# Turning normalised rows on TensorE instead of by DMA transpose, with a new opening, in a transformer block of two FFNs around attention

## The chip, the cores and the metric

The kernel runs on one core of one Trainium2 chip. The metric is device time in microseconds (us), measured over whole executions; the median of three runs of the kernel before is 693.76 us. One execution was also taken with the hardware profiler. Its span, from the first to the last instruction, is a little shorter than its time.

The engines are named as in the profile: PE is TensorE (matmuls; PEld is its weight loads), DVE is VectorE, ACT is ScalarE, POOL is GpSimd, and SP is SyncE, which here only issues DMAs.

## What is computed

The input x has 32 batches of 256 rows with 128 features. The reference, cut to its steps:

```
x = x + 0.5 * ffn(layernorm(x))
x = x + attn(layernorm(x))
x = x + 0.5 * ffn(layernorm(x))

ffn(h):   h = concat([h, -h]);  h = s0 * (h @ sign(k0));  h = 2 * relu(h)
          h = s1 * (h @ sign(k1));  h = 2 * relu(h);  return s2 * (h @ sign(k2))
attn(h):  Q, K, V = h @ W.T + b  in 16 heads of 8 features
          ctx = softmax(Q K^T / sqrt(8)) V
          return layernorm(ctx + h) * gamma + beta
```

Here sign(k) is +1 where the boolean k is true and -1 elsewhere, and the hidden widths are 512 and 512. The result is float32. Products keep its precision by splitting each operand in a float16 high part and a float16 low part, and adding two or three products.

## The kernel before

**Units and stages.** The rows are cut into 16 units of two batches: 512 rows, held as a tile of 128 partitions by 4 row groups by 128 features. Each unit passes through ffn0 (`first`), the attention norm (`norm_attn`), the projections (`project`), and per batch the score maxima (`maxima`), their transport (`shift`), the weighted sum (`weigh`) and the end of attention (`context`), and then ffn1 (`second`; the last unit does it in two halves).

**Normalising and turning.** `normalize` (L544) computes row statistics on VectorE (L557, L558), the inverse root on POOL (L559, L561), and then subtracts and multiplies, on VectorE if `quick` (L566) and else on POOL (L571, L572). `turned` (L574) makes the turned tile xT, with features on partitions, in two float16 parts. If `quick`, TensorE transposes float32 row groups into PSUM (L585), ACT casts the high part (L588) and VectorE subtracts for the low part (L589). Else ACT casts (L593) and POOL subtracts (L594) first, and SP issues one DMA transpose of both parts (L595). The quick path is used for ffn0 of units 0 and 1 (QF = 2), the attention norm of unit 0 (QK = 1), and ffn1 of units 14 and 15 (QL = 2).

**Feed-forward.** `ffn` makes two hidden layers of four blocks and an output. Each block's product lands in one of three PSUM buffers named "m", which the projections, the transposes and the context share. `relu_split` (L618) evicts it: ACT writes the high part (L625), VectorE the low part (L626); or ACT writes a float32 copy (L628) and POOL subtracts (L623). The last residual addition is on VectorE (L678) or on ACT and POOL (L679, L680).

**Attention.** `project` (L709) makes Q and K (L384 to L386, evictions L728 and L730) and places them by DMA through DRAM (L733, L738) in a tile where a head has 8 of 32 partitions, three rows of parts and a fourth row for the shift. Q is a fresh tile for each unit, and its fourth row of 32 partitions is first filled with zeros by DMA from a DRAM tile (L717). `maxima` runs score matmuls (L781) and takes the row maxima on VectorE (L792). `shift` (L796) splits the maxima in a float16 high part (L802) and low part (L803) on VectorE, TensorE turns them (L809), ACT copies them (L814), and two DMAs put them in Q's fourth row (L815, L816), so that the second score product (L849) has the shift in it. ACT takes the exponential (L861), TensorE multiplies by V and a column of ones (L831), and `context` turns the result (L875), divides (L887, L888), adds, normalises and adds to x (L890 to L895, on VectorE if `quick`, else on POOL).

**The order of the work.** `_Plan` sets it. Every operation is recorded with an engine, an estimated cost and a rank, and `simulate` (L154) plays the engines against each other and writes the order of each engine's queue. TensorE takes its groups by rank and may skip ahead by SKIP or SKIP0. Score products of a batch and weighted ones of an earlier batch with the same rank run together. The array is used in three tilings: "D" (128x128), "C" (four blocks of 32 columns) and "R" (four blocks of 32 rows, for scores). Dense products (`dense`, L380) can run in "D" or "C" and take the tiling that is in use. `relief` (L259) moves a low part from VectorE to ACT and POOL where the simulation says that it ends sooner. A unit's stages have ranks at a distance of UNIT = 16 between units, with offsets: B0 for ffn0, BA for the attention norm, BP for the projections, BW for the weighted sums, B1 for ffn1, and AHEAD for how far a norm precedes its products. The loads of x are on SP at ranks two units ahead (L608).

**The opening.** x of unit 0 is loaded in halves, then the scalars, k0, k1, unit 1's x and k2. POOL sets the blank tiles of V and K to their constants (`blanks`, L530). The weights are unpacked on VectorE and ACT (`weights`, L406). `projections` (L454) scales, turns and splits the attention weights; the biases of Q and K are loaded a second time as rows (L476) and permuted on POOL (L490).

Of the kernel before, what the change touches and what calls it, by code (L numbers as in the profile page):

```python
# [55 lines left out]
PT, NHL, NXN = 5, 3, 5  # L56
# [3 lines left out]
QL = 2  # L60
# [5 lines left out]
B0, BA, BP, BW, BV, B1 = -34, -12.449, -7.379, 13, 4, 42.542  # L66

S0, S1 = 0.0, -1.082

BB = 2.143  # L70

RUSH, AHEAD = 0.378, 4.629

SKIP0, SKIP, UNTIL = 30.226, 3.003, 20.423

FAR = 37.851
# [3 lines left out]
WAIT = 0.12  # L80
# [8 lines left out]
BIAS = 0.6  # L89
# [18 lines left out]
class _Node:  # L108
    __slots__ = ("n", "eng", "cost", "emit", "rank", "kind", "rows", "lag", "needs", "then", "bufs", "count", "avail", "start", "tiling", "alt", "rush")


class _Plan:
# [11 lines left out]
    def op(self, eng, cost, emit, r=(), w=(), rank=0.0, kind="D", rows=0, lag=None, alt=None, rush=False):  # L124
# [3 lines left out]
        x.then, x.avail, x.start, x.rush = [], 0.0, None, rush  # L128
        needs = set()
# [24 lines left out]
    def simulate(self):  # L154
# [104 lines left out]
        def relief(now, best):  # L259

            nonlocal left
            for x in sorted((x for x in ready[DVE] if x.alt and x.avail <= now + 1e-9), key=lambda x: (x.rank, x.n)):
# [10 lines left out]
                y.rush, y.needs, y.then, y.bufs, y.count, y.avail, y.start = False, [], [x], [source, temp], 0, 0.0, None  # L273
# [18 lines left out]
            return None  # L292

        mode = "D"
        while left:
# [8 lines left out]
            while again:  # L304
                again = False
                for eng in range(5):
# [15 lines left out]
                    if group:  # L322
                        begin(group, now)
                        again = True
# [28 lines left out]
def tile_macaron(ctx: ExitStack, tc: tile.TileContext, x, Wq, bq, Wk, bk, Wv, bv, gamma, beta, k0, k1, k2, s0, s1, s2, out):  # L353
# [49 lines left out]
    op(POOL, 0.6, lambda: make_identity(nc, ident), w=["ident"], rank=-900)  # L403
    op(ACT, 1.58, lambda: nc.scalar.copy(ident16, ident), r=["ident"], w=["ident16"], rank=-850)

    def weights():  # L406
# [10 lines left out]
        sc1 = const.tile([P, 2], F32, name="sc1")  # L417
        for i, (src, e, eng) in enumerate(((s0, ACT, nc.scalar), (s1, SP, nc.sync), (s2, SP, nc.sync))):
            op(e, 0.5, lambda i=i, src=src, eng=eng: eng.dma_start(out=raw[:, i : i + 1], in_=src.partition_broadcast(P)),
               w=[("raw", i)], rank=-901, lag=3.2)  # L420
        op(ACT, 0.5, lambda: nc.scalar.dma_start(out=k0s.t, in_=k0.rearrange("(c p) f -> p c f", p=P)), w=[k0s], rank=-900, lag=2.6)
        op(ACT, 0.53, lambda: nc.scalar.dma_start(out=k1s.t, in_=k1.rearrange("(c p) f -> p c f", p=P)), w=[k1s], rank=-899, lag=3.2)
# [10 lines left out]
        for c in range(NF):  # L433
            if c < NF - 1:
                op(ACT, 0.7, lambda c=c: nc.scalar.activation(w1[:, c, :], k1s.t[:, c, :], AF.Identity, scale=sc1[:, 0:1], bias=sc1[:, 1:2]),
                   r=[k1s, "sc1a", "sc1b"], w=[("w1", c)], rank=-800)
            else:
                v(0.4, lambda c=c: nc.vector.tensor_scalar(w1[:, c, :], k1s.t[:, c, :], -0.5, sc1[:, 0:1], ALU.add, ALU.mult),
                  [k1s, "sc1a"], [("w1", c)])
        v(0.4, lambda: nc.vector.tensor_scalar(w2, k2s.t, 2.0, -1.0, ALU.mult, ALU.add), [k2s], ["w2"], B0 + 2)  # L440
        v(0.1, lambda: nc.vector.tensor_tensor(sab, raw, sgn, ALU.mult), [*raws, "sgn"], ["sab"], B0 + 2)
# [12 lines left out]
    def projections():  # L454
# [4 lines left out]
        br = const.tile([1, 2, 2, P], F32, name="br")  # L459
# [12 lines left out]
        for i, (W, b) in enumerate(((Wq, bq), (Wk, bk), (Wv, bv))):  # L472
            s(lambda i=i, W=W: nc.sync.dma_start(out=ws[:, i, :], in_=W), [("ws", i)])
            s(lambda i=i, b=b: nc.sync.dma_start(out=bn[:, i : i + 1], in_=b.rearrange("(f o) -> f o", o=1)), [("bn", i)])
            if i < 2:
                s(lambda i=i, b=b: nc.sync.dma_start(out=br[:, i, 0, :], in_=b.rearrange("(o f) -> o f", o=1)), [("br", i)])  # L476
# [5 lines left out]
        v(0.45, lambda: nc.vector.tensor_tensor(sq[:, :, 0:D], ws, ws, ALU.mult), wss, ["sq"])  # L482
        v(0.1, lambda: nc.vector.scalar_tensor_tensor(sq[:, :, D], bn, 1.0 / 128, bn, ALU.mult, ALU.mult), bns, ["sqb"])
# [8 lines left out]
        for i in range(2):  # L492
            op(POOL, 0.5, lambda i=i: permute(br[:, i, 1, :], br[:, i, 0, :], nc.gpsimd.tensor_copy), r=[("br", i)], w=[("brp", i)], rank=B0 + BB)
# [14 lines left out]
        def turn():  # L508
            for i in range(3):
                nc.tensor.transpose(pw.t[:, i, :], ws[:, i, :], ident)  # L510
            for i in range(2):
                nc.tensor.matmul(pw.t[:, 3, i : i + 1], br[:, i, 1, :], ones[0:1, 0:1], start=True, stop=True)

        op(PE, 0.7, turn, r=[*wss, "ident", ("brp", 0), ("brp", 1), "ones"], w=[pw], rank=B0 + BB + 0.3)
# [13 lines left out]
    nought = dram.tile([32, G, TU], F16, name="nought", bufs=1)  # L528

    def blanks():  # L530
        for j in range(NV):
            rank = j * UNIT + BP - 12
            op(POOL, 1.35, lambda j=j: nc.gpsimd.memset(vaug[j], 0.0), w=[("V", j)], rank=rank)
            op(POOL, 0.95, lambda j=j: nc.gpsimd.memset(ks[j].bitcast(I32), ONES), w=[("K", j, row) for row in range(4)], rank=rank)
# [5 lines left out]
        zero = buf(work, [32, G, TU], F16, "pt", PT, "zero")  # L540
# [3 lines left out]
    def normalize(dst, src, tag, n, rank, scale=1.0, quick=False):  # L544
# [7 lines left out]
        for a in range(0, n, step):  # L552
# [8 lines left out]
            op(POOL, 0.25 + 0.2 * step, lambda part=part: nc.gpsimd.tensor_tensor(rs.t[:, part, 0], ve.t[:, part], nhalf[:, part], ALU.pow),  # L561
# [12 lines left out]
    def turned(xn, tag, name, n, rank, quick):  # L574

        xT = buf(work, [P, 2, n * P], F16, f"xT{tag}", 2, f"xT{name}")
# [14 lines left out]
        else:  # L591
            hl = buf(work, [P, 2, n, D], F16, "hl", NHL, f"hl{name}")
            op(ACT, 0.52, lambda: nc.scalar.copy(hl.t[:, 0], xn.t), r=xns, w=[(hl, 0)], rank=rank)  # L593
            op(POOL, 1.12, lambda: nc.gpsimd.tensor_tensor(hl.t[:, 1], xn.t, hl.t[:, 0], ALU.subtract), r=[*xns, (hl, 0)], w=[(hl, 1)], rank=rank)  # L594
            op(SP, 1.35, lambda: nc.sync.dma_start_transpose(  # L595
                out=xT.t.rearrange("p a (t q) -> p (a t) q", q=P), in_=hl.t.rearrange("p a t d -> p (a t d)")),
               r=[(hl, 0), (hl, 1)], w=[(xT, i, a) for i in range(2) for a in range(0, n, 2)], rank=rank, lag=3.5)
        return xT

    xs, xns, qs, xTs, nms, cxs = {}, {}, {}, {}, {}, {}  # L600

    def load(u):
# [5 lines left out]
        e, eng, rank = (ACT, nc.scalar, -898) if u == 1 else (SP, nc.sync, (u - 2) * UNIT + B0)  # L608
        op(e, 0.5, lambda: eng.dma_start(out=b.t.rearrange("p (b c) d -> p b c d", b=2), in_=xu[u]), w=[(b, 0), (b, 2)], rank=rank, lag=2.7)


    def norm_ffn(key, src, n, rank, quick):
# [3 lines left out]
        xTs[key] = turned(xn, key[0][-1], name, n, rank, quick)  # L616

    def relu_split(hi, lo, m, ps, w, rank):  # L618
# [3 lines left out]
        def low(of):  # L622
            return lambda: nc.gpsimd.tensor_tensor(lo.t[:, m, :], of.t, hi.t[:, m, :], ALU.subtract)  # L623

        op(ACT, 0.09 + w / 1280, lambda: nc.scalar.activation(hi.t[:, m, :], ps.t, AF.Relu), r=[ps], w=[(hi, m)], rank=rank)  # L625
        op(DVE, 0.08 + w / 985, lambda: nc.vector.scalar_tensor_tensor(lo.t[:, m, :], ps.t, 0.0, hi.t[:, m, :], ALU.max, ALU.subtract),  # L626
           r=[ps, (hi, m)], w=[(lo, m)], rank=rank,
           alt=(0.09 + w / 1280, lambda: nc.scalar.activation(full.t, ps.t, AF.Relu), ps, full, 0.1 + w / 500, low(full)))  # L628

# [52 lines left out]

    def first(u):
        rank = u * UNIT + B0 + S0 * u / (NU - 1)
        norm_ffn(("ffn0", u), (xs[u], 0), NT, rank - AHEAD if u else -950, u < QF)
        ffn(("ffn0", u), (xs[u], 0), NT, rank, UNIT)

    def second(u, b):
        n, part = (NT, 0) if b is None else (2, 2 * b)
        rank = u * UNIT + B1 + S1 * u / (NU - 1) + (b or 0) * UNIT / 2  # L690
        norm_ffn(("ffn1", u, b), (xs[u], part), n, rank - AHEAD, u >= NU - QL)
        dsts = ffn(("ffn1", u, b), (xs[u], part), n, rank, UNIT * n / NT)
# [203 lines left out]


    load(0)
    weights()
    load(1)  # L900
    projections()
    blanks()
    for u in range(NU):
        if u > 1:
            load(u)
# [44 lines left out]
```

## Time and profile before

| what | value |
| --- | --- |
| median of 3 runs | 693.76 us (691.03 to 695.23) |
| profiled execution, its time | 695.02 us |
| profiled execution, its span | 693.2 us |
| PE, DVE, ACT, POOL busy | 644.7, 600.2, 536.6, 458.8 us |
| first dense matmul | at 12.44 us |
| first score maxima | at 49.7 us |
| DMA transposes on SP | 43, median 1.24 to 1.28 us each |

The busy time of an engine is the sum over its instructions, and waits are not in it. A row of a table of groups gives the line, the engine, the operation and its tiles, then the count, the busy time, the mean length of one, and the idle time before it. Matmuls overlap: the length of one is longer than the distance to the next start, so a spacing is read from starts. A row of waits has the engine and line that waited, for whom, then the us in total, the times and the longest.

### The profile page before, as it was taken

How to read it: one execution, taken by the hardware profiler on the slowest of the kernel's cores; microseconds unless marked ns; L12 is line 12 of the kernel's file. 1: busy time of each engine (PE TensorE's matmuls, PEld its weight loads, DVE VectorE, ACT ScalarE, POOL GpSimd, SP SyncE). 2: the span in 40 equal slices, each digit the busy share in tenths (PEclk: the TensorE clock that was granted, in tenths of full speed). 3: DMA queues.
4: the chain of work that ended last, by engine and by line, in shares of the span. 5: the costliest groups of instructions: out<-in, count | busy, mean ns of one | idle time of the engine just before them, and what ended most of it. 6: DMA issues, size and time to landing. Idle time of an engine off the chain costs nothing.

```text
span 693.2 us, 29847 instructions
## 1 busy us (share of the span) xinstructions
PE 644.7 (93%) x13082; PEld 330.4 (48%) x13082; DVE 600.2 (87%) x1227; ACT 536.6 (77%) x792; POOL 458.8 (66%) x585
## 2 busy tenths in 40 slices
PE   3989879899999999999999999999999998988997
PEld 1544434545455454545445454544545453543445
DVE  6879988889989888999988898999989888888675
ACT  3545867888889787988888788887878887877773
POOL 6766677679595958869594978866474967653110
PEclk9999979999999999999999999999999999999999
DMA  5142342323333141313323143322213151302000
GB/s 155 45 110 64 73 126 19 103 50 97 56 64 98 26 133 35 111 44 72 94 42 113 34 112 43 70 71 59 75 20 117 22 115 24 88 26 35 5 17 31
DMA packets 79398, 46.69 MB, mean 67 GB/s; under 512 B 50562, under 2 KB 74628, under 8 KB 79268
## 3 DMA queue, kind: packets, MB, share of 16 engines
q1 hardware_dynamic: 77380, 43.93, 26.5%
q8 instruction: 102, 1.67, 1.0%
q10 hardware_dynamic: 1888, 0.85, 0.5%
q14 instruction: 28, 0.23, 0.1%
HBM read 20.25 MB, written 13.24 MB: 48 GB/s over the span
## 4 chain that ended last, share of the span: by engine, by line
PE 70%; DVE 15%; ACT 9%; issue 3%; DMA 2%; SPq 1%; ACTq 0%; POOL 0%
PE p_None L386 17%; PE cx L831 15%; PE p L386 15%; PE sc L849 7%; DVE nm L792 5%; ACT pt L861 5%; PE p L383 4%; PE nat L781 3%; PE p_None L383 2%; PE tp L875 2%; DVE mt L803 2%; PE pv L386 1%; ACT qkhl L728 1%; DVE qkhl L730 1%; PE pq L383 1%
## 5 line engine op out<-in xcount | busy, mean ns | idle before, releaser
L792 DVE TENSOR_REDUCE nm<-nat 128x4 f32<-128x1024 f32 x256 | 310.8, 1217 | 35.7 <-PE nat L781 31.5
L861 ACT ACTIVATE pt<-sc,esc 128x1024 f32<-128x1024 f32 x256 | 285.7, 1118 | 71.4 <-PE nat L781 59.2
L386 PEld LDWEIGHTS <-w 128*32 128x32 f16 x4048 | 103.5, 96 | 97.6 <-issue 31.0
L831 PE MATMUL cx<-pt,vaug 128*32 128x256 f32 x2048 | 139.0, 389 | 0.0
L849 PE MATMUL sc<-Q,ks 32*128 32x256 f16 x1024 | 105.1, 275 | 12.6 <-ACT pt L861 12.2
L781 PE MATMUL nat<-ks,Q 32*128 32x256 f16 x1024 | 102.0, 274 | 2.6 <-ACT pt L861 1.3
L386 PE MATMUL p<-h1h,w 128*32 128x512 f16 x860 | 87.0, 383 | 0.1
L386 PE MATMUL p<-h1l,w 128*32 128x512 f16 x860 | 86.3, 380 | 0.0
L386 PE MATMUL p_None<-h1h_None,w 128*32 128x512 f16 x800 | 80.6, 382 | 0.9 <-ACT full L628 0.8
L831 PEld LDWEIGHTS cx<-pt,vaug 128*32 128x32 f32 x2048 | 59.0, 110 | 47.0 <-issue 16.7
L386 PE MATMUL p_None<-h1l_None,w 128*32 128x512 f16 x800 | 80.4, 379 | 0.3 <-issue 0.3
L849 PEld LDWEIGHTS <-ks 32*128 32x128 f16 x1024 | 32.9, 92 | 71.4 <-issue 65.8
L625 ACT ACTIVATE h2h<-p 128x512 f16<-128x512 f32 (+1 forms) x72 | 41.1, 572 | 22.1 <-PE p L383 11.8
L625 ACT ACTIVATE h1h<-p 128x512 f16<-128x512 f32 (+1 forms) x72 | 40.3, 575 | 14.8 <-PE p L383 10.5
L781 PEld LDWEIGHTS <-Q 32*128 32x128 f16 x1024 | 32.1, 92 | 39.1 <-issue 38.3
L626 DVE SCALAR_TENSOR_TENSOR h2l<-p,h2h 128x512 f16<-128x512 f32 (+1 forms) x63 | 41.0, 651 | 10.5 <-ACT h2h L625 10.3
L559 POOL TENSOR_SCALAR ve_a<-mv_a 128x4 f32<-128x4 f32 (+1 forms) x17 | 3.3, 194 | 69.0 <-PE sc L849 40.5
L383 PEld LDWEIGHTS <-w 128*128 128x128 f16 x308 | 29.6, 100 | 29.4 <-issue 10.5
L626 DVE SCALAR_TENSOR_TENSOR h1l<-p,h1h 128x512 f16<-128x512 f32 (+1 forms) x59 | 38.1, 655 | 4.5 <-ACT h1h L625 4.2
L625 ACT ACTIVATE h2h_None<-p_None 128x512 f16<-128x512 f32 x60 | 35.7, 595 | 6.9 <-PE p_None L386 4.2
L625 ACT ACTIVATE h1h_None<-p_None 128x512 f16<-128x512 f32 x60 | 34.5, 605 | 5.4 <-PE p_None L386 5.3
L386 PE MATMUL p_None<-xT_None,w 128*32 128x512 f16 x480 | 36.6, 390 | 0.9 <-issue 0.6
(159 smaller groups left out, 1376.5 us busy)
## 6 DMA issues: line engine op xcount, KB each, us to landing
dr<-qkhl SPq DMA_DIRECT2D x32, 256.0 KB
Q<-dr SPq DMA_DIRECT2D x48, 128.0 KB
ks<-dr SPq DMA_DIRECT2D x48, 128.0 KB
out_dram<-x SPq DMA_DIRECT2D x15, 256.0 KB
x<-in_L_attn_x_dram SPq DMA_DIRECT2D x14, 256.0 KB
Q<-nought SPq DMA_DIRECT2D x16, 128.0 KB
dm<-mr SPq DMA_DIRECT2D x32, 16.0 KB
Q<-dm SPq DMA_DIRECT2D x32, 16.0 KB
```

Of the source, the lines that this page charges most:

```text
L383: nc.tensor.matmul(to, w, of, start=start, stop=stop)
L386: nc.tensor.matmul(to[32 * r : 32 * r + 32], w[:, 32 * r : 32 * r + 32], of, start=start, stop=stop)
L625: op(ACT, 0.09 + w / 1280, lambda: nc.scalar.activation(hi.t[:, m, :], ps.t, AF.Relu), r=[ps], w=[(hi, m)], rank=rank)
L626: op(DVE, 0.08 + w / 985, lambda: nc.vector.scalar_tensor_tensor(lo.t[:, m, :], ps.t, 0.0, hi.t[:, m, :], ALU.max, ALU.subtract), r=[ps, ( ...
L728: op(ACT, 0.586, lambda i=i, pq=pq, hl=hl: nc.scalar.activation(hl.t[:, 0, :], pq.t, AF.Identity, bias=bs[:, i : i + 1]), r=[pq, "bs"], w= ...
L781: nc.tensor.matmul(nat.t[:, ii, qc, :], Q.t[32 * r : 32 * r + 32, g, b * S + qc * P : b * S + qc * P + P], K[32 * r : 32 * r + 32, g, b * ...
L792: op(DVE, 1.141, lambda g=g, pr=pr, nat=nat: nc.vector.tensor_reduce(nm.t[:, :, 2 * pr : 2 * pr + 2, g].rearrange("p q i -> p i q"), nat.t ...
L803: op(DVE, 0.12, lambda: nc.vector.scalar_tensor_tensor(mt.t[:, :, :, 1, :], nm.t, 1.0 / ONE, mt.t[:, :, :, 0, :], ALU.mult, ALU.subtract), ...
L831: nc.tensor.matmul(cx.t[32 * r : 32 * r + 32, g // 2, :], V[:, 2 * b + kc, 4 * (g // 2) + r, 16 * (g % 2) : 16 * (g % 2) + 32], pts[g, r / ...
L849: nc.tensor.matmul(sc.t[:, ii, kc, :], K[32 * r : 32 * r + 32, g, b * S + kc * P : b * S + kc * P + P], Q.t[32 * r : 32 * r + 32, g, b * S ...
L861: op(ACT, 1.012, lambda pt=pt, sc=sc: nc.scalar.activation(pt.t, sc.t, AF.Exp, scale=esc), r=[sc, "esc"], w=[pt], rank=rank - RUSH, rush=True)
L875: nc.tensor.transpose(tp.t[:, qc, 8 * c : 8 * c + 8, :].rearrange("p h n -> p (h n)"), cxT.t[:, c, bass.ts(qc, P)], ident)
```

## The change

- `TURNED = '01a'` makes every call of `turned` take the TensorE path: all ffn0, ffn1 and attention norms. The other path is rewritten (32x32 transposes on VectorE and a way through DRAM), but no call reaches it. A turn has a rank LATE = 0.943 behind its norm.
- `shift` computes the high part on ACT, and the low part in two steps on POOL.
- Q has three fixed tiles, set to zero once on POOL. From the fourth unit on only the shift's 8 rows are set to zero by DMA.
- The loads of all x follow each other on SP in the opening (ranks -708 to -675).
- Unit 0's norm and turn come ahead of the weights' work: blanks on POOL and some of the weights' work on VectorE now depend on them. k0 is loaded first of the weights; w1's blocks go to VectorE, ACT and twice POOL. The biases are permuted by a product with a permuted identity.
- TensorE runs 24 matmuls on the identity as soon as that is there (`WARM`).
- `divert` lets the planner send a ReLU's eviction to ACT as a float32 copy, with both the float16 cast and the subtraction on POOL.
- The constants of the planner are new. Among them QL = 0 puts the norms and contexts of the last units on POOL, B0 goes from -34 to -30, FAR from 37.851 to 19.271, and ffn1's rank has a step after unit 0.

```
-PT, NHL, NXN = 5, 3, 5
+PT, NTB, NTF, NXN = 5, 2, 2, 5
-QL = 2
+QL = 0
-B0, BA, BP, BW, BV, B1 = -34, -12.449, -7.379, 13, 4, 42.542
+B0, BA, BP, BW, BV, B1 = -30, -11.087, -6.172, 13, 4, 42.202
+P0, P1, P2, SLOW = 15.998, 17.354, 16, 1
+TURNED, LATE = '01a', 0.943
+WARM = 24
-BB = 2.143
+BB = 15.813
-RUSH, AHEAD = 0.378, 4.629
+RUSH, AHEAD = -0.12, 4.08
-SKIP0, SKIP, UNTIL = 30.226, 3.003, 20.423
+SKIP0, SKIP, UNTIL = 10.311, 2.868, 24.337
-FAR = 37.851
+FAR = 19.271
-WAIT = 0.12
+WAIT = 0
...
+        def divert(x, now):
+            low, evict, full, cost, cast, sub, rest = x.pair
...
+            if max(free[POOL], end + 0.2) + wait + cost + sub > max(free[DVE], end) + before + low.cost + BIAS2 or not fits(x, [full]):
+                return
...
+            x.emit, x.then = evict, [y]
...
+            low.eng, low.cost, low.emit, low.alt = POOL, sub, rest, None
...
+        def spin():
+            for _ in range(WARM):
+                nc.tensor.matmul(warm.t, ident, ident, start=True, stop=True)
+        op(PE, 0.22 * WARM, spin, r=["ident"], w=[warm], rank=-960)
...
     def turned(xn, tag, name, n, rank, quick):
+        quick = quick or tag in TURNED
...
-            op(SP, 1.35, lambda: nc.sync.dma_start_transpose(
...
-        e, eng, rank = (ACT, nc.scalar, -898) if u == 1 else (SP, nc.sync, (u - 2) * UNIT + B0)
+        e, eng, rank = (ACT, nc.scalar, -898) if u == 1 else (SP, nc.sync, u - (690 if u > 3 else 710))
...
-        Q = buf(work, [P, G, TU], F16, "Q", 3, f"Q_{u}")
+        Q = qs[j]
...
+        if u >= NV:
+            op(SP, 0.4, lambda: nc.sync.dma_start(out=Q.rearrange("(x j) g n -> j x g n", j=16)[3], in_=nought), r=["nought"], w=[("S", j, 0), ("S", j, 1)], rank=rank - 2, lag=2)
...
-        op(DVE, 0.2, lambda: nc.vector.tensor_scalar(mt.t[:, :, :, 0, :], nm.t, 1.0 / ONE, None, ALU.mult), r=nmr, w=[(mt, 0)], rank=rank)
-        op(DVE, 0.12, lambda: nc.vector.scalar_tensor_tensor(mt.t[:, :, :, 1, :], nm.t, 1.0 / ONE, mt.t[:, :, :, 0, :], ALU.mult, ALU.subtract),
-           r=[*nmr, (mt, 0)], w=[(mt, 1)], rank=rank)
+        op(ACT, 0.2, lambda: nc.scalar.mul(mt.t[:, :, :, 0, :], nm.t, 1.0 / ONE), r=nmr, w=[(mt, 0)], rank=rank)
+        op(POOL, 0.25, lambda: nc.gpsimd.tensor_scalar(ns.t, nm.t, 1.0 / ONE, None, ALU.mult), r=nmr, w=[ns], rank=rank)
+        op(POOL, 0.3, lambda: nc.gpsimd.tensor_tensor(mt.t[:, :, :, 1, :], ns.t, mt.t[:, :, :, 0, :], ALU.subtract), r=[ns, (mt, 0)], w=[(mt, 1)], rank=rank)
```

## The prediction, made before the result was known

> **What bounds the kernel now.** I read the busy times and the 40 slices first, then the table of windows by stage, then single instructions on TensorE, then the waits, and the chain last.
>
> The head of the page:
>
> ```profile
> span 693.2 us, 29847 instructions
> PE 644.7 (93%) x13082; PEld 330.4 (48%) x13082; DVE 600.2 (87%) x1227; ACT 536.6 (77%) x792; POOL 458.8 (66%) x585
> PEclk9999979999999999999999999999999999999999
> ```
>
> TensorE is the fullest engine, VectorE next, and the clock is low in one slice (87 to 104 us). An average hides stages, so the next view cuts the span in stretches (columns: length, busy us of PE, PEld, DVE, ACT, POOL, granted clock, DMA share, GB/s):
>
> ```profile
> 0.00:20.00 20.00, 9.19 (x25) 3.44 (x26) 13.42 (x53) 7.06 (x12) 12.53 (x25) 1.00 0.54 148
> ...
> 60.00:110.00 50.00, 42.28 (x880) 20.52 (x872) 43.23 (x85) 35.09 (x49) 31.45 (x37) 0.90 0.33 84
> ...
> 306.60:345.70 39.10, 38.48 (x847) 19.86 (x847) 35.65 (x72) 33.15 (x49) 29.82 (x37) 1.00 0.33 75
> ...
> 612.10:645.40 33.30, 27.38 (x468) 13.13 (x468) 27.87 (x50) 24.14 (x32) 14.08 (x19) 0.95 0.13 20
> ...
> 665.50:693.30 27.80, 21.64 (x240) 15.68 (x229) 17.38 (x45) 10.91 (x27) 3.82 (x7) 1.00 0.06 20
> ```
>
> 306.6 to 345.7 is one unit (two batches) of the steady state, from its first maxima to the next unit's. From 148 to 580 us eleven units take 39.3 us each, and TensorE is busy 98% of one. So there added TensorE work adds time, and relief of another engine adds nothing. The opening, 60 to 110 us and the end have room on TensorE.
>
> How a turn on TensorE is priced, from the kernel's own float32 transposes (start, length, what):
>
> ```profile
> 301.26 0.39 PE L386 MATMUL p_None<-h1l_None,w 128*32 128x512 f16 x4
> 301.58 0.66 PE L875 MATMUL tp<-ident,cxT 128*128 128x128 f32 x4
> 302.07 0.59 PE L383 MATMUL p<-xT,w 128*128 128x512 f16 x2
> ```
>
> Four take 0.49 us from start to start, plus 0.10 for entering their tiling (0.32 us after a group that otherwise takes 0.22). Between dense neighbours (24.84 to 25.28 us) four took 0.44.
>
> The waits that the change touches:
>
> ```profile
> PEld L809 <- DVE mt L803: 18.3, 25, 1.4
> PE pm L809 <- DVE mt L803: 8.8, 14, 1.1
> ...
> SPq L595 <- POOL fxn L571: 74.5, 8, 10.2
> ...
> L803 DVE SCALAR_TENSOR_TENSOR mt<-nm,mt x32: 166/898/1167, 60.6 to 647.1; 128x32 f16<-128x32 f32 x32
> ```
>
> TensorE stands 8.8 us for shift's second part. That instruction has 32 elements a row; its shortest is 166 ns and its median 898, so most of it is waiting inside. SP sits at the DMA transposes with its later transfers behind them, but in the steady state nothing on TensorE waits for a DMA.
>
> **The change, part by part.** The sum is made against the profiled execution: 695.0 us with a span of 693.2. The median of three is 693.8, so the profiled one stands 1.3 above it.
>
> *Turns.* 43 of 49 row groups went through a DMA transpose (14 ffn0, 15 attention, 14 ffn1). All 43 now go to TensorE: four transposes each, 0.44 us between dense neighbours, 0.59 with an entry, and 0.74 if the two halves stand apart between scores (two transposes at 650.5 us cost 0.37). I take 0.53, nearer the 0.59 row because the steady state is mostly in the narrow tilings: 43 x 0.53 = 22.8 us, with ends 18.8 and 31.8. Seven of the 43 (ffn0 of units 2 and 3, attention of 1 to 3, ffn1 of 12 and 13) fall where TensorE has room. That leaves 36 x 0.53 = +19.1 on the path.
> On the other engines a turn gives ACT 2 x 0.37 in place of one cast of 0.62, VectorE 2 x 0.42 in place of nothing, and takes 1.16 from POOL and a 1.27 us transpose instruction from SP. ACT +0.4 and VectorE +2.5 us a unit hide behind TensorE only while VectorE, at 35.7 of 39.1, is given something back; the next item does that. Each turn also takes one of three PSUM buffers, which is a rival below.
>
> The skill differs on price. "TensorE: Matmul & The Clock Gate", Part 4, puts a 128x128 transpose in a kernel's context at about 275 ns. This trace shows 273 ns as the length of one (L875) but 109 ns from one start to the next, because they overlap. Priced by that page's figure, four in a row would be 1.1 us and 43 turns 47 us, an estimate that would make the kernel some 7% slower. The measured spacing decides.
>
> *Shift.* VectorE loses L802 (8.7 us) and L803 (21.3 us), 30.0 in all, against 43 x 0.84 = 36.1 for the turns. The last units' contexts and norms also leave VectorE for POOL, about 12 us by their rows (L566, L890, L893 to L895), and the planner may now divert a ReLU's low part to POOL, which lost 43 x 1.16 = 50 us. VectorE is about even in the steady state.
> ACT's part is near its small copies (0.22 to 0.35), POOL's two near L538's 0.24 and below L571's 0.61. Behind the ACT part wait exponentials, behind POOL's the normalisations; pm on TensorE waits for both. At best the 8.8 us go. At worst a running POOL instruction (up to 1.27) and an exponential (1.12) stand ahead, and TensorE stops 0.5 us longer in each of 32: +16. I take -6: a 1 us surprise in the VectorE part is what made the stall, and the two engines' queues are what the planner counts itself.
>
> *Opening.* POOL's first norm step waits until 5.83 us behind memsets (vaug at 4.37, 1.37 long), the first row turn is at 8.6, and the first dense matmul at 12.44. The memsets now follow the norm, and the weights' VectorE work that stood between (1.1 and 0.9 us) follows the turn. From the statistics' end at 4.7: norm 1.0, two rows 0.6, turn 0.5, cast 0.4, and the second half one step of 0.9 later with its 0.4 subtract puts dense work at about 9: -3.4. The matmuls of 13.3 to 18.4 us start 0.43 us apart, and 0.22 after it. That is the half clock; 24 spins ahead of it should spare 2.5. Ends: 0 (k1s lands at about 7.7, and the w1 parts on POOL, 2 of about 1 us, or k0s come late) and -8. I take -5.5.
> All x loads go ahead on SP: two of 0.5 us stand before the attention weights and twelve behind. Those weights are wanted only at 38 us, which hides them; the stretch's DMA share of 0.54 leaves room for the 3.5 MB. The zeros for Q are needed only from the fourth unit, and the biases' row loads become one product with a permuted identity; both cost nothing while the first projections stand at 38 us. Three memsets of Q (0.94 each) lie on POOL under the same cover.
>
> The same page (Part 1) says the array's clock opens after about 3.4 us of sustained work; here it opened at 18.4, 5.1 us after dense work began. By the page the spins, at 0.22 us each when cold, open it before any product. Part 4 adds that transposes do not count as such work, which speaks against more of them in a stretch as thin as 90 to 107 us; no run yet shows that.
>
> *Front stretch.* 20 to 148 us. With each matmul counted at its steady spacing (0.216 us per 512 columns, four narrow ones together) and 0.1 per change of tiling, some 28 us of this stretch are not work. The half clock takes 5 of them (0.51 in 90 to 93.5 us, 0.52 in 100 to 107). Without DMA transposes ahead in SP's queue, Q and K of unit 1 arrive earlier: in the chain K lands only from 72.6 to 75.1, and unit 1's maxima start at 75.7. Ends +5 (the turns' evictions crowd VectorE) and -12; I take -6, the dip and one more.
>
> *End.* The last context and norm run on POOL: an addition 0.73 for 0.42, two norm steps 1.23 for 0.60, three more at 0.73 for 0.42, and the ffn's two at 1.22 for 0.59. That is +2.5, less about 0.7 in which VectorE was taken by h2l: +1.8 (ends 0 and +4). The later rank of second() moves about two slots of ffn work behind the attention; TensorE's work is the same, so I leave it at 0.
>
> Sum: 19.1 - 6 - 5.5 - 6 + 1.8 = +3.4 on 695.0, so 698.4 for a like execution, and 697.2 against the median, 1.3 lower: I say 697.
>
> **Rivals.**
> *Faster: VectorE and SP were the front's and end's limit.* In 60 to 110 us VectorE is busy 43.2 of 50, and in 612 to 645 it is 27.9 of 33, with POOL at 14. If the freed POOL takes low parts off it (six at 0.68 make 4 us at the end) and SP no longer holds Q and K back, the front gives its full 12 (6 more than taken), the end 4, the opening 8 (2.5 more) and shift 8.8 (2.8 more): 697 - 15.3 = 682. It decides once these shorten the run by over 10 us more than I took. Against it: VectorE gets the turns' subtractions in the same stretches.
> *Slower: PSUM.* The three buffers take about 25 fills a unit; now 28. Each turn holds one from its first transpose through cast and subtract, over 1.3 us. If TensorE finds no buffer for 0.5 us at each of 36 turns, 697 + 18 = 715. It decides from about 0.2 us a turn. For it: there is no slack at 98% busy. Against it: TensorE hardly waits for buffers now.
> *The shift doesn't get cheaper*: ACT and POOL make pm wait as long as VectorE did. 697 + 6 = 703.
>
> **How the numbers follow.** Forecast 0.38 (own range 690 to 703), faster rival 0.26, PSUM 0.22, shift 0.14. A measurement here can tell about 1% from no change, that is below 686.8 or above 700.7. Faster: 0.25 of the faster rival and 0.01 of the forecast, 0.26. Slower: 0.22, 0.08 of the shift's 0.14, and 0.03 of the forecast, 0.33. Same: 0.41. The range 680 to 714 leaves out a quarter of the faster rival and under half of PSUM's.
>
> **What would show it.** Right: a steady unit of about 40.3 us with the transposes' starts 0.11 apart; L809's wait under 3 us; the first dense matmul near 9 us at 0.22 spacing; first maxima near 44. Wrong: steady units at or under 39.3 (the turns found room that I don't see), or over 41 with TensorE idle before transposes or products (PSUM); an opening that still starts dense work at 12; a front without the dip in the clock, which gives 5 us by itself.

## The result, and the profile after

| | before | after |
| --- | --- | --- |
| median, measured together | 692.39 us (690.72 to 695.23) | 703.62 us (703.43 to 704.36) |
| ratio | | 1.016 [1.012, 1.020] |
| profiled execution: time, span | 695.02, 693.2 us | 703.43, 701.6 us |

The change made the kernel 1.6% slower, 11.2 us by the medians and 8.4 us by the spans. The forecast was 697, with "within 1%" likeliest. The time lies in the range 680 to 714, but 0.6 us above the forecast's own range, and on the side that had a chance of 0.33.

The head of the page after:

```profile
span 701.6 us, 29624 instructions
PE 669.6 (95%) x12940; PEld 349.4 (50%) x12940; DVE 585.5 (83%) x1187; ACT 547.2 (78%) x873; POOL 499.0 (71%) x689
PEclk9899998999999999999999999999999999999999
```

TensorE gained 25 us of busy time (7.8 of them the spin), VectorE lost 15, and POOL gained 40. The clock is now low in two slices, one of them in the opening. The table of windows after (columns as in the prediction: length, busy us of each engine, granted clock, DMA share, GB/s), cut at the first maxima, a steady unit and the last maxima:

```profile
0.00:20.00 20.00, 14.21 (x70) 10.17 (x70) 11.91 (x39) 6.62 (x13) 10.84 (x21) 0.91 0.69 205
20.00:57.10 37.10, 29.88 (x192) 15.66 (x196) 28.29 (x76) 15.89 (x37) 22.60 (x33) 0.91 0.20 63
...
310.70:350.70 40.00, 40.00 (x864) 20.80 (x857) 34.96 (x73) 34.44 (x55) 30.70 (x42) 1.00 0.14 44
...
652.90:701.60 48.70, 42.97 (x560) 25.70 (x554) 23.33 (x62) 28.59 (x49) 26.38 (x45) 1.00 0.06 18
```

A steady unit takes 40.0 us where it took 39.3, and TensorE has no idle time left in it by this view. VectorE has come down from 35.7 to 35.0.

To split the difference I counted TensorE's records in both traces at their steady spacing ("work": 0.216 us per 512 columns, double for float32, a quarter where four blocks share the array), added 0.097 us for each change of tiling, and called what is left of a stretch "rest". The spin is left out of the work.

| stretch | before: us = work + switches, rest | after | difference |
| --- | --- | --- | --- |
| start to first maxima | 49.7 = 29.1 + 2, 20.4 | 57.1 = 28.7 + 2, 28.2 | +7.4 |
| to unit 3's maxima | 98.5 = 66.6 + 90, 23.3 | 93.8 = 66.3 + 93, 18.6 | -4.7 |
| units 3 to 14 | 432.0 = 370.6 + 365, 26.0 | 439.5 = 386.2 + 404, 14.2 | +7.5 |
| unit 14 to the last maxima | 65.1 = 44.1 + 61, 15.1 | 62.4 = 46.3 + 67, 9.6 | -2.7 |
| to the end | 47.8 = 35.1 + 25, 10.3 | 48.7 = 36.6 + 25, 9.7 | +0.9 |

So TensorE got 18.6 us of work and 48 switches (4.7 us) more, 23.3 in all, and its rest fell by 14.8. The one place where the rest grew is the opening.

The turns in the steady state, in the timeline after (start, length, what):

```profile
303.78 0.38 PE L420 MATMUL p_None<-h1l_None,w 128*128 128x512 f16 x1
304.00 0.60 PE L632 MATMUL t<-ident,fxn 128*128 128x128 f32 x4
304.43 0.38 PE L420 MATMUL p_None<-h1h_None,w 128*128 128x512 f16 x1
```

Four transposes take 0.43 us from start to start, 0.108 each, as the row of before had it. The waits that answer to L809's:

```profile
PEld L874 <- POOL mt L869: 2.7, 5, 1.0
...
PE pm L874 <- POOL mt L869: 0.5, 1, 0.5
```

and the rows of shift's instructions (min/median/max ns):

```profile
L867 ACT ACTIVATE mt<-nm x32: 219/230/266, 67.0 to 654.1; 128x32 f16<-128x32 f32 x32
L869 POOL TENSOR_TENSOR mt<-ns,mt x32: 251/252/256, 67.4 to 654.6; 128x32 f16<-128x32 f32 x32
```

The wait for the low part fell from 8.8 to 0.5 us on the products and from 18.3 to 2.7 on the loads. On VectorE that part took 166 to 1167 ns; on POOL it takes 251 to 256.

The opening, in the timeline after (lines of the queues, SPq and ACTq, are the issue of a DMA):

```profile
1.38 7.79 PE L446 MATMUL warm<-ident 128*128 128x128 f32 x48 [1.38 <-POOL ident masks.py:199]
...
3.41 0.43 ACTq L666 DMA_DIRECT2D x<-in_L_attn_x_dram  x1
...
9.01 0.38 PE L632 MATMUL t<-ident,fxn 128*128 128x128 f32 x2
...
10.48 0.29 DVE L603 BATCH_NORM_STATS2 st_f<-x 128x6 f32<-128x128 f32 x1 [1.94 <-DMA x<-in_L_attn_x_dram]
10.75 0.60 DVE L612 TENSOR_SCALAR fxn<-x,mv_f,rs_f 128x128 f32<-128x128 f32 x2
11.24 0.49 PE L632 MATMUL t<-ident,fxn 128*128 128x128 f32 x2 [1.84 <-DVE fxn L612]
```

Unit 0's first half is normalised by 6.5 us, but the spin holds TensorE until 9.0. The second half waits for VectorE, which stands at unit 1's x: that was issued at 3.41 and landed at 10.45. So dense work starts at 12.72, where it started at 12.44. Then comes the longest stop:

```profile
16.42 7.98 DVE L612 TENSOR_SCALAR fxn<-x,mv_f,rs_f 128x128 f32<-128x128 f32 x4
...
18.88 1.39 POOL L576 MEMSET vaug<- 128x1536 f32 x1
20.19 0.96 POOL L577 MEMSET ks<- 128x1024 int32 x1
21.09 0.95 POOL L584 MEMSET qs<- 128x1024 f32 x1
21.98 1.38 POOL L576 MEMSET vaug<- 128x1536 f32 x1
23.30 0.95 POOL L577 MEMSET ks<- 128x1024 int32 x1
...
24.39 0.69 PE L632 MATMUL t<-ident,fxn 128*128 128x128 f32 x2 [5.64 <-DVE fxn L612]
```

Four norm steps of unit 1, whose shortest is 0.34 us, take 7.98 us on VectorE, and the last two of them (6.50 and 5.46 us by themselves, begun at 17.83 and 18.95) end 0.1 us after POOL's five memsets in a row. TensorE stands 5.64 us for them.

### The profile page after: what moved, and what is told of

The parts are those of the page before. It is cut to its first block, busy times and chain, and to the rows that moved or that the text cites. A ratio compares the mean times of both kernels' runs of the same rounds, so it can differ in the third digit from the quotient of the medians.

```text
span 701.6 us, 29624 instructions
## 1 busy us (share of the span) xinstructions
PE 669.6 (95%) x12940; PEld 349.4 (50%) x12940; DVE 585.5 (83%) x1187; ACT 547.2 (78%) x873; POOL 499.0 (71%) x689
## 4 chain that ended last, share of the span: by engine, by line
PE 77%; DVE 9%; ACT 6%; POOL 3%; DMA 2%; issue 2%; SPq 1%; ACTq 0%; DVEq 0%; POOLq 0%
PE p_None L423 17%; PE p L423 16%; PE cx L896 15%; PE sc L914 8%; PE p L420 5%; DVE nm L855 4%; PE p_None L420 4%; ACT pt L926 3%; PE nat L844 3%; PE pq L423 2%; PE tp L940 2%; DMA x<-in_L_attn_x_dram 1%; PE ta L632 1%; DVE fxn L612 1%; PE pv L423 1%
## 5 line engine op out<-in xcount | busy, mean ns | idle before, releaser
L423 PEld LDWEIGHTS <-w 128*32 128x32 f16 x3984 | 95.4, 96 | 100.9 <-issue 32.6
L914 PE MATMUL sc<-qs,ks 32*128 32x256 f16 x1024 | 104.3, 274 | 6.9 <-ACT pt L926 5.6
L844 PE MATMUL nat<-ks,qs 32*128 32x256 f16 x1024 | 101.2, 274 | 3.2 <-ACT pt L926 1.9
L896 PEld LDWEIGHTS cx<-pt,vaug 128*32 128x32 f32 x2048 | 58.5, 110 | 48.7 <-issue 16.4
L423 PE MATMUL p<-h1h,w 128*32 128x512 f16 x764 | 75.4, 382 | 0.2 <-DVE xT_None L636 0.2
L423 PE MATMUL p<-h1l,w 128*32 128x512 f16 x764 | 74.9, 379 | 0.0
L914 PEld LDWEIGHTS <-ks 32*128 32x128 f16 x1024 | 32.0, 92 | 71.5 <-issue 65.1
L955 POOL TENSOR_TENSOR y<-y,axn 128x256 f32<-128x256 f32 x32 | 23.4, 730 | 39.5 <-DVE y L953 38.7
L683 DVE SCALAR_TENSOR_TENSOR h2l_None<-p_None,h2h_None 128x512 f16<-128x512 f32 x50 | 34.2, 684 | 18.2 <-ACT h2h_None L682 18.2
L683 DVE SCALAR_TENSOR_TENSOR h2l<-p,h2h 128x512 f16<-128x512 f32 (+1 forms) x53 | 34.6, 654 | 16.8 <-ACT h2h L682 16.6
L420 PEld LDWEIGHTS <-w 128*128 128x128 f16 x324 | 31.3, 101 | 29.6 <-issue 13.0
L844 PEld LDWEIGHTS <-qs 32*128 32x128 f16 x1024 | 31.6, 92 | 26.3 <-issue 24.3
L680 POOL TENSOR_TENSOR h1l<-full,h1h 128x512 f16<-128x512 f32 (+1 forms) x30 | 33.9, 1132 | 3.8 <-ACT full L685 2.8
```

Of the source, the lines that this page charges most:

```text
L420: nc.tensor.matmul(to, w, of, start=start, stop=stop)
L423: nc.tensor.matmul(to[32 * r : 32 * r + 32], w[:, 32 * r : 32 * r + 32], of, start=start, stop=stop)
L683: l = op(DVE, 0.08 + w / 985, lambda: nc.vector.scalar_tensor_tensor(lo.t[:, m, :], ps.t, 0.0, hi.t[:, m, :], ALU.max, ALU.subtract), r=[p ...
L844: nc.tensor.matmul(nat.t[:, ii, qc, :], Q[32 * r : 32 * r + 32, g, b * S + qc * P : b * S + qc * P + P], K[32 * r : 32 * r + 32, g, b * S ...
L896: nc.tensor.matmul(cx.t[32 * r : 32 * r + 32, g // 2, :], V[:, 2 * b + kc, 4 * (g // 2) + r, 16 * (g % 2) : 16 * (g % 2) + 32], pts[g, r / ...
L914: nc.tensor.matmul(sc.t[:, ii, kc, :], K[32 * r : 32 * r + 32, g, b * S + kc * P : b * S + kc * P + P], Q[32 * r : 32 * r + 32, g, b * S : ...
```

## The experiments

Theory: the turns cost some 0.5 us each on TensorE, shift's move gives part of that back, and the opening loses what the front gains. Rivals: the planner's order or constants make the difference and the turns are free; or the opening alone is to blame. The kernels of e1 to e4, of e5 to e8 and of e9 to e12 each ran on one chip with their own runs of before, whose medians were 692.07, 692.62 and 693.0 us.

**e1: the change without the turns.** The DMA transposes return to the kernel after.

```
-TURNED, LATE = '01a', 0.943
+TURNED, LATE = '', 0.0
...
+            op(SP, 1.35, lambda: nc.sync.dma_start_transpose(
...
```

> The changed kernel with one part undone: the turns go by DMA transpose again, as in the kernel before (cast on ACT, subtraction on POOL, one DMA transpose on SP), and nothing else. Theory 'TensorE work': 43 turns cost 23 us of TensorE (0.44 us each and about 0.1 us for the tiling), 36 of them in the saturated stretch, so the steady unit falls from 40.0 to 38.3-38.8 us and the whole to 682-690 us. Rival 'the turns are free, the loss is the opening and the new order': the steady unit stays at 39.8 us or more and the whole within 2 us of 703.5.

Measured: 718.56 us, 1.038 [1.034, 1.043]. Both were wrong. TensorE's work fell by 19.4 us as it should (46 turns go by DMA here, since QL = 0 stays), but its rest in units 3 to 14 rose from 14.2 to 39.2 us, and the waits of e1 show one reason:

```profile
PEld L864 <- POOL mt L859: 15.5, 15, 1.9
...
PE pm L864 <- POOL mt L859: 11.4, 11, 1.6
```

POOL has the subtractions of the turns again, and they stand ahead of shift's. The planner makes a new order for the new operations, but with constants (offsets, ranks, biases) that suit others. So a part taken out with the constants left as they are measures the order too. e7 mends that.

**e2: the change with shift on VectorE.**

```
-        op(ACT, 0.2, lambda: nc.scalar.mul(mt.t[:, :, :, 0, :], nm.t, 1.0 / ONE), r=nmr, w=[(mt, 0)], rank=rank)
-        op(POOL, 0.25, lambda: nc.gpsimd.tensor_scalar(ns.t, nm.t, 1.0 / ONE, None, ALU.mult), r=nmr, w=[ns], rank=rank)
...
+        op(DVE, 0.2, lambda: nc.vector.tensor_scalar(mt.t[:, :, :, 0, :], nm.t, 1.0 / ONE, None, ALU.mult), r=nmr, w=[(mt, 0)], rank=rank)
...
```

> The changed kernel with shift's two parts back on VectorE, and nothing else. Theory 'the part on VectorE is stretched while POOL runs and TensorE waits for it': 6 to 9 us slower (709-713 us), TensorE's waits for the transposed maxima back above 8 us, the second part's median length near 0.9 us. Rival 'the wait was covered or moves elsewhere': within 2 us of 703.5.

Measured: 722.16 us, 1.043 [1.039, 1.047], which is 18.5 more than after; a steady unit takes 40.0 to 43.0, on average 41.1. The sign is the theory's, the size is not, and the two other signs that were expected did not come: the low part takes 182 ns in the median on VectorE here (898 in before), and TensorE stands for it 2.5 us on the products and 4.7 on the loads. So most of the 18.5 us is not that wait. The rest in units 3 to 14 grew by 13 us; what makes it up wasn't traced, and this one too holds an order with constants for other work.

**e3: before with shift on ACT and POOL**, the reverse edit, nothing else.

> The kernel before with shift's parts on ACT and POOL, and nothing else. Theory: 5 to 9 us faster than before (683-687 us), steady unit 38.5-38.9 us, and the wait before the transposed maxima nearly gone. Rival 'ACT and POOL queues make TensorE wait as long as VectorE did': within 2 us of 692.4.

Measured: 691.33 us, 0.997 [0.994, 1.000]. Unit 14's maxima come 8.0 us earlier (572.3 for 580.3), with the rest in units 3 to 14 at 17.6 for 26.0; from there to the end it takes 118.7 for 112.9 us. So the move is worth 8 us in the steady state, and 5.8 are given back behind it. The wait for the low part, expected to be nearly gone, only went down: from 8.8 to 4.4 us on the products and from 18.3 to 11.9 on the loads.

**e4: before with all turns on TensorE.**

```
     def turned(xn, tag, name, n, rank, quick):
+        quick = True
...
-FAR = 37.851
+FAR = 19.271
```

The ranks of ffn's and the attention's turns also get after's 0.943.

> The kernel before with all turns on TensorE at a rank 0.943 behind their norm, and FAR at 19.271, without which its plan has no order. Theory 'TensorE work': steady unit 40.6-41.0 us, whole 709-716 us. Rival 'free': steady unit 39.3 us, whole within 4 us of 692.4 (FAR may move it a little).

Measured: 727.43 us, 1.051 [1.047, 1.055]. The work rose by 18.5 us, and the rest in units 3 to 14 from 26.0 to 37.7. Again more than the theory, and again with an order for other work; e11 repeats it fairly.

**e5: every transpose of every turn issued twice**, in the order of the kernel after; the second writes the same values again.

```
                         nc.tensor.transpose(pt.t[:, bass.ts(t, P)], xn.t[:, t, :], ident)
+                        nc.tensor.transpose(pt.t[:, bass.ts(t, P)], xn.t[:, t, :], ident)
```

> The changed kernel with every transpose of a turn issued twice (49 turns, the second into the same place), with the planner's costs unchanged, so that the order of every engine stays as it was. The output is unchanged. It prices a turn with no new order. Theory 'TensorE work decides': 45 of the 49 lie where TensorE is full, 0.44 us each, so 703.5 + 15 to 21 = 719-725 us and the steady unit at 41.2-41.5. Rival 'turns find room': less than 8 us slower.

Measured: 724.06 us, 1.045 [1.040, 1.049]: 20.4 more than after, 0.42 us for each of the 49 turns. A steady unit takes 41.3, which is 1.3 for three turns. This is the cleanest price, because the order is the same: of the 0.43 us that four transposes take in a row, 0.42 came out on the path.

**e6: the first zeros on ACT.** The zeros of two V and two Q tiles are written by ACT; the order is the same.

```
...
-            op(POOL, 0.95, lambda j=j: nc.gpsimd.memset(qs[j].bitcast(F32), 0.0), r=["normed", ("w1", 3)],
+            op(POOL, 0.95, lambda j=j: nc.scalar.mul(qs[j].rearrange("p g n -> p (g n)"), nhalf[:, 0:1].broadcast_to([P, G * TU]), 0.0) if j < 2 else nc.gpsimd.memset(qs[j].bitcast(F32), 0.0), r=["normed", ("w1", 3)],
```

> The changed kernel with the zeros of two V tiles and two Q tiles in the opening written by ACT (idle there for 7.5 us) in place of POOL, at the same places of the order. Theory 'VectorE's two norm steps of unit 1, 6.5 and 5.5 us long, wait for a pause of POOL, which runs five blank instructions without one': these two end 2-4 us earlier, the first score maxima come 2-4 us before 57.1, the whole 700-702 us. Rival 'they wait for the data or for SP's loads': lengths and first maxima unchanged within 1 us.

Measured: 699.58 us, 1.010 [1.007, 1.013], 4.0 less than after; the first maxima come at 52.3 for 57.1. The norm steps of unit 1 in e6, with two memsets left on POOL (19.12 to 20.97 us):

```profile
16.82 4.55 DVE L612 TENSOR_SCALAR fxn<-x,mv_f,rs_f 128x128 f32<-128x128 f32 x4
```

They are 3.4 us shorter, and the two long ones end again as POOL's memsets end. So the zeros on POOL were worth 4 us of the opening's loss.

**e7: e1 with the planner's constants searched anew**, that is, chosen for the order that ends first by the planner's own costs. The core of its diff to e1:

```
-QL = 0
+QL = 1
...
-BB = 15.813
+BB = 18.369
-RUSH, AHEAD = -0.12, 4.08
+RUSH, AHEAD = -0.244, 4.832
-SKIP0, SKIP, UNTIL = 10.311, 2.868, 24.337
+SKIP0, SKIP, UNTIL = 15.326, 2.888, 24.337
...
```

> The changed kernel with the turns by DMA transpose (as in the first experiment) and the planner's constants searched anew for it (B0, BP, B1, P0, LATE, BB, RUSH, AHEAD, SKIP0, SKIP, BIAS, BIAS2, QL). Theory 'TensorE work decides, and the first experiment was slow because its order was made for other work': steady unit 38.3-39.0 us, whole 684-692 us. Rival 'the new shift, divert and DMA turns do not go together on POOL': steady unit above 40 us, whole above 703 us.

Measured: 688.99 us, 0.9955 [0.993, 0.998]. Nearly the same instructions as in e1 (13244 products for 13315, 711 instructions on POOL in both, 44 turns by DMA for 46) in another order are 29.6 us faster, and the kernel after without its turns is 14.6 faster than with them, although the first maxima come as late (58.1). A steady unit of e7, in the table of windows:

```profile
227.70:266.60 38.90, 38.90 (x892) 19.50 (x888) 33.72 (x68) 33.42 (x51) 34.07 (x48) 1.00 0.37 71
```

**e8: e3 with the constants searched anew.**

```
-QL = 2
+QL = 1
...
-SKIP0, SKIP, UNTIL = 30.226, 3.003, 20.423
+SKIP0, SKIP, UNTIL = 30.448, 3.003, 17.125
...
-BIAS = 0.6
+BIAS = 0.756
```

> The kernel before with shift's parts on ACT and POOL and the planner's constants searched anew for it (BA, BP, B1, S0, S1, BB, RUSH, AHEAD, SKIP0, UNTIL, FAR, WAIT, BIAS, QL). Theory 'shift's new place is worth 8 us in the steady state, and only the end, ordered for other costs, gave it back': 681-687 us, steady unit 38.2-38.6. Rival 'the end gives it back whatever the order': 690 us or more.

Measured: 685.28 us, 0.989 [0.985, 0.994]. One edit of the change, with constants searched for it, beats both kernels. A steady unit of e8:

```profile
263.50:301.60 38.10, 38.10 (x851) 19.41 (x847) 33.87 (x66) 33.48 (x51) 32.14 (x42) 1.00 0.31 81
```

The constants of before were not searched anew with its own work, so how much of the 7 us is the search and how much the move isn't separated here; the 8 us of the steady state in e3 came without a search.

**e9: no spin.**

```
-WARM = 24
+WARM = 0
```

> The kernel after without the 48 matrix products that spin TensorE up; nothing else differs. Theory: the spin gains nothing, since the clock it opens (full from 6.0 us) closes again at 12.8, just as the dense work begins, and TensorE's first row turn waits behind it from 6.5 to 9.0 us. But the second half's norm is ready only at 10.75, held by unit 1's x, so only the first half's turn moves: first dense matmul at 12.2 to 12.7 us, first maxima within 1 us of 57.1, time 702 to 704.5. Rival: the spin spares a half clock before 12.8; without it the clock stays low until about 18 to 20 us, the first maxima come 1.5 to 3 us later, time 705 to 707.

Measured: 703.79 us, 1.016 [1.012, 1.019], the time of after. TensorE in e9:

```profile
5.79 0.73 PE L632 MATMUL t<-ident,fxn 128*128 128x128 f32 x2 [5.79 <-DVE fxn L612]
11.40 0.69 PE L632 MATMUL t<-ident,fxn 128*128 128x128 f32 x2 [4.88 <-DVE xT L636]
12.55 1.90 PE L420 MATMUL p<-xT,w 128*128 128x512 f16 x4 [0.46 <-ACT xT L635]
```

The first turn is 3.2 us earlier, the second not, and the first four products take 1.90 us, 0.43 apart, just as in after. So the spin neither costs nor gains in this opening.

**e10: x loaded one unit ahead, as before.**

```
-        e, eng, rank = (ACT, nc.scalar, -898) if u == 1 else (SP, nc.sync, u - (690 if u > 3 else 710))
+        e, eng, rank = (ACT, nc.scalar, -898) if u == 1 else (SP, nc.sync, (u - 2) * UNIT + B0)
```

> The kernel after with the later units' x loads issued where the kernel before issues them, one unit ahead of use; the order is otherwise the same. Theory: with twelve x loads fewer in the front of the queues, unit 1's x lands before 10.45 us (by about 8), VectorE no longer stands 1.94 us for it, the first dense matmul is at about 11 us and the first maxima 1 to 2 us earlier than 57.1; time 701.5 to 703. Rival: the weights' landing, or VectorE behind GpSimd's memsets, sets the first maxima anyway; time 703 to 704.5 with first maxima within 0.5 us. Slower than 705 would say that loading all x at once did help the front.

Measured: 701.0 us, 1.012 [1.008, 1.016], 2.8 less than e9 beside it and 2.6 less than after; none of its runs (up to 702.71) reaches one of e9's (from 702.89). TensorE in e10:

```profile
10.52 1.70 PE L420 MATMUL p<-xT,w 128*128 128x512 f16 x6 [0.99 <-ACT xT L635]
...
15.02 0.38 PE L420 MATMUL p<-h1l,w 128*128 128x512 f16 x1
15.53 0.30 PE L632 MATMUL t<-ident,fxn 128*128 128x128 f32 x1
21.86 0.90 PE L632 MATMUL t<-ident,fxn 128*128 128x128 f32 x3 [6.03 <-DVE fxn L612]
22.55 0.63 PE L420 MATMUL p<-h1h,w 128*128 128x512 f16 x1
```

Unit 1's x is used at 8.05 instead of 10.48 us, dense work starts 2.2 earlier and at the full rate, since it now follows the spin closely. The first maxima come at 54.9. The stop behind the memsets is still there, 6.03 us long, and after it the products start at half rate again.

**e11: e4 with the constants searched anew**, among them QF = 1 and QL = 0.

> The kernel before with all 49 turns on TensorE and nothing else of the change, with the planner's constants searched anew for it (in the earlier run of this edit they were not, and it took 727.4). Theory: the turns alone cost 0.44 to 0.53 us each on the path, 16 to 19 for 36 of them, and VectorE, which keeps shift's parts, holds TensorE some more: 706 to 714, steady unit 40.3 to 41. Rival: the turns need shift taken off VectorE, or the buffers in PSUM run short whatever the order: over 718, with steady units over 41.5 and TensorE idle over 2.5 us in each.

Measured: 711.32 us, 1.027 [1.023, 1.032]. That is 18.3 more than before: the price of the turns alone. The work rose by 18.6 us in all, and the rest in units 3 to 14 only from 26.0 to 28.1. A steady unit of e11:

```profile
313.10:354.30 41.20, 40.44 (x846) 20.68 (x838) 38.65 (x80) 33.01 (x51) 25.72 (x34) 1.00 0.17 53
```

VectorE, which makes the turns' low parts here and shift's too, is at 38.65 of 41.2: the second bound that shift's move takes away. The first maxima come at 47.1 us here (46.1 in e4), with the opening of before and the turns on TensorE.

**e12: e7 with the opening mended**: e6's zeros on ACT, e9's and e10's edits.

> The retuned kernel after with DMA transposes (689.0 us), and its opening mended by what the runs pointed to: the zeros of the first two vaug and Q tiles written by ACT, x loaded one unit ahead as before, no spin; order otherwise the same. Theory: the opening's gains do not depend on the turns, so the 4 us of the zeros come again, and 0 to 3 more of the other two: 682 to 686, first maxima at 50 to 54 us. Rival: the front of this version is set by its DMA transposes, as in the kernel before, and takes the gain back by unit 3: 687 to 690 although the first maxima come earlier.

Measured: 683.84 us, 0.987 [0.984, 0.991], 5.2 less than e7, the fastest kernel of the study by its median (e8's runs, 682.88 to 688.34, overlap with its 682.82 to 685.0). TensorE's opening in e12:

```profile
5.69 0.73 PE L632 MATMUL t<-ident,fxn 128*128 128x128 f32 x2 [5.69 <-DVE fxn L612]
9.25 0.69 PE L632 MATMUL t<-ident,fxn 128*128 128x128 f32 x2 [2.83 <-DVE xT L636]
10.39 3.79 PE L420 MATMUL p<-xT,w 128*128 128x512 f16 x8 [0.46 <-ACT xT L635]
```

Dense work starts at 10.39 and the first maxima come at 48.9, 9.2 earlier than in e7. By the spans, 681.0 and 688.4, 7.4 of them are left at the end.

## Why the prediction was right or wrong

**Turns (+19.1 on the path): right.** Work and switches rose by 23.3 us, where 43 x 0.53 = 22.8 were put down (the lower end there, 43 x 0.44, is 18.9 and not 18.8). On the path they cost 18.3 us from the side of before (e11), and 14.6 for 44 of them from the side of after (e7), both with constants searched for the order; doubled in place they cost 0.42 each (e5), which is 18 for 43, with no search in it. So 0.53 was a little high: of 32 turns between 150 and 590 us that I looked up, 8 stand between dense neighbours, as at 304.00, and 21 are entered from a narrow tiling but followed by dense products, which share the one switch. The skill's 275 ns for a transpose ("TensorE: Matmul & The Clock Gate", Part 4) is again the length of one, 273 ns here, and e5 says what one more costs in a row of them: 0.42 / 4 = 0.105 us.

**Shift (-6): right in kind, small in size.** I took the 8.8 us that TensorE stood for the low part as the most that could go. In units 3 to 14 the rest fell by 11.8 us in after and by 8.4 in e3, where nothing but the move (and what order the planner made of it) differs. In e3 the row of that wait fell by only 4.4 us, half of what the rest gained, so the wait that carries the instruction's name was not the whole of its price. That VectorE's 21.3 us in L803 also held back everything behind it in its queue would explain the other half; no run separates it. The sentence that in the steady state "relief of another engine adds nothing" fell with this: e3 took work off VectorE and none off TensorE.

**Opening (-5.5): wrong, the step that failed.** It came out at +7.4, 12.9 us off, more than the whole miss (5.0 by the spans): dense work began at 12.72 and not at about 9, at half rate, and stopped again at 18.7. The loss is the new opening's and not the turns': e11 and e4 keep the opening of before, turn everything on TensorE, and have their first maxima at 47.1 and 46.1 us, 10 us ahead of after. Three statements failed:
- "All x loads go ahead on SP [...] the stretch's DMA share of 0.54 leaves room for the 3.5 MB." Room over 20 us is not room for the one transfer that VectorE waits for: unit 1's x took 7.04 us from issue to landing, and e10 gives 2.6 us back by loading the others later, of which the two that SP issued from 2.10 to 3.94 us had gone ahead of it.
- "Three memsets of Q (0.94 each) lie on POOL under the same cover." The cover was counted for TensorE's products at 38 us, not for VectorE beside POOL at 17 us. POOL's zeros now stand in one row of five at 18.88 to 24.25 us, and VectorE's norm steps stand with them. e6 takes three of the five away and gains 4.0 us.
- "24 spins ahead of it should spare 2.5." They spare nothing (e9). They last 7.79 us and not the 5.3 that 24 x 0.22 gives: a product is two records, which start 0.21 us apart until the clock opens at 6.0 us and 0.11 after it, so 0.22 is the price of a product at the full clock and 0.43 that of a cold one. And the clock that they open closes again as the dense work comes, 3.6 us after them.

The last two points can be read together: after the stop at 18.7 to 24.4 us the products start 0.43 us apart again, until 29.6. The clock was granted 0.5 from 23.0 to 29.8. In e6, where the stop is 1.95 us, it stays open. The rule that an idle window of some 3.4 us closes the clock ("TensorE: Matmul & The Clock Gate", Part 1) agrees with both. That transposes don't count as work for it (Part 4) is shown by no run here: in after the clock closed at 12.78 although two pairs of transposes left no idle time over 1.84 us between the spin and the dense work, but these pairs are short, and a window that is only mostly idle would explain it too.

**Front (-6): the size came, -4.7; its cause is not shown.** Between units 1 and 2 the rest fell from 14.4 to 9.2 us; it is 10.3 in e11, where nothing but the turns and the constants changed, and 15.0 in e7, with DMA transposes. So the turns do take rest out there, by SP's queue or by POOL's subtractions. But their own work comes in its place: to unit 3's maxima e11 takes 101.0 us for the 98.5 of before, and e7 takes 94.0 for the 93.8 of after. This stretch is short in after, e6, e7, e9, e10 and e12 (92.6 to 94.6 us; 96.2 in e1, 99.2 in e2), whichever way the turns go, and which of the other edits or constants shortens it wasn't separated. Of the 10.2 us at half clock in before, 6.8 stayed (104.9 to 111.8 us), so the gain is not "the dip and one more".

**End (+1.8): wrong in sign and small**, -2.7 + 0.9 = -1.8 us, although the end holds turns of its own. Which edit shortened it wasn't separated.

By the spans: predicted -5.5 - 6 + (19.1 - 6) + 1.8 = +3.4, measured +7.4 - 4.7 + 7.5 - 1.8 = +8.4. The opening's 12.9 were covered in part by 5.6 too much for the steady state and 3.6 for the end, while the front gave 1.3 less than was put down. So the total was nearer than its terms.

**The rivals.** *PSUM* (715) did not come: the rows in which a turn stands for an eviction (ACT's and VectorE's) add up to 2.9 us in the whole run, under the 7.2 (36 x 0.2) from which it was to decide, and the rest fell. *Shift not cheaper* gave 703, the number that came, by a mechanism that e3 and the waits of after refute; a time that fits does not make its reason right. *Faster* needed 10 us more from front, end, opening and shift: the steady state and the end gave 9.2, and the opening took 12.9.

**What is open.** With the opening mended (e12) the first maxima come at 48.9 and not at the 44 that I had put down for dense work at 9 us; products at half rate until 15.7 are part of it, the rest wasn't traced. e12 leaves the spin out, while in e10 dense work behind the spin ran at the full rate from 10.5 us; whether a spin pays once x comes early wasn't run. And what a search of the constants would do for before and after themselves wasn't run, so e11's 18.3 and e7's 14.6 may hold some of it.

## What to carry to other kernels

Work added to the engine that is busy 98% of a stage comes out at its full spacing, however short one instruction looks, and relief of another engine can give back more than the waits that carry its name. An opening is read instruction by instruction: which transfer and which instruction of a neighbour engine each step stands for, and not by shares of a stretch. Where a planner makes the order, take a part out only with its constants chosen again; left alone they turned -14.6 us into +15.

## What the runs showed of the hardware

- **VectorE behind POOL's row of memsets.** A norm step of 0.34 us took 6.50 us in after (17.83 to 24.33) while POOL ran a subtraction until 18.94 and then five memsets one after another; it ended only when the row of memsets did, and so it was in e10 (6.50 us) and, behind two memsets, in e6 (3.02). The skill ("SBUF — State Buffer", Who interferes with whom) says that a VectorE instruction of this kind and a GpSimd instruction can shut each other out for the length of an instruction. The trace goes further: the longest memset is 1.39 us, and VectorE did not get in between two of them. Between two subtractions in a row just before it did: the norm step ahead ended at 17.91, 0.08 us after the first of these.
- **The granted clock and the rate.** In e9 the granted clock reads 1.00 from 10 to 20 us, but products start 0.43 us apart until 14.67 and 0.21 from 15.3. The first change of the clock that this trace holds is the rise at 15.25 us, so before it the view says nothing, and the spacing is to be trusted.
- **Nearly the same instructions, another order:** 29.6 us, 4%, between e1 and e7, more than any part of the change.
